# Loading the last stage's inputs during the last image's layer 3, into tiles that earlier stages leave

## The chip, the cores and the metric

The kernel runs on one core of one Trainium2 chip. The metric is device time in microseconds, and the median of several runs counts. TensorE (PE) multiplies into PSUM, VectorE (DVE) and ScalarE (ACT) do the elementwise work, GpSimd (POOL) does small corrections and some copies, and SyncE (SP) issues nearly all DMA transfers, which run on 16 DMA engines.

## The reference

The input is x, 16 images of 64 channels, 128 x 128, float32. Four residual layers follow each other; `gn` is a group norm without parameters over 32 groups of two channels.

```python
x = x + conv1x1(gram(gn(x)) @ gn(x))            # layer 0: a 64 x 64 Gram matrix per image
x = x + |sobel_x(gn(x))| + |sobel_y(gn(x))|     # layer 1: depthwise
x = x + conv3x3(shift(gn(x))) + b               # layer 2: a quarter of the channels shifted left, one right
v = conv1x1(conv3x3(gn(x), w_bin)) + b1         # layer 3
mean, var = v.mean((0, 2, 3)), v.var((0, 2, 3)) # over all 16 images
v = (v - mean) * rsqrt(var + 1e-5) * gamma + beta
x = x + clip(leaky_relu(v), 0, 255)
```

Layer 3's statistics run over the whole batch. So its final normalisation and addition can only begin when the convolution of the last image is done.

## The kernel before

The work has two parts. The first goes through the images in a software pipeline. A step handles one group of 8 rows of each image half (R = 8, NS = 8 groups per image), and each step has four quarters q. In one step the pipeline works on up to four images: `Gram` (the Gram matrix of a later image), `Front` (layers 0 and 1), `Layer2` and `Layer3`. They start at fixed offsets: image b has its layer 3 in steps 35 + 8b to 43 + 8b. All engines are wrapped in `InOrder` (line 72), so each engine keeps the order in which the program issues.

During the last image's layer 3 (from step 155 on) no other stage has work left. A group i of that layer takes one step:

- q = 0: PE forms the shared product and half of the others, from `v3`.
- q = 1: PE forms the other half; ACT normalises the next group from the layer's inputs (`x3` tiles, a ring of 10 of which an image holds 8); SP stores the previous group's `y` to `y_d` in four transfers (line 835).
- q = 2: DVE adds the products into a `y` tile (ring of 2, line 839), then forms differences of the next group, for which PE waits.
- q = 3: more differences, and ACT squares y for the statistics.

Layer 3's input of every image was stored to the DRAM tensor `x3_d` earlier, by layer 2. All SBUF pools of this part are opened in a `with ExitStack() as ph` block (line 157), so their memory is free again when it ends.

The second part, here called the end, starts with a short chain of small operations on the sums (`mv`, `pm_bn`, `sc`, `sh`). Then it streams over everything: for each of 64 pieces it loads y and the layer's input, applies scale, shift and relu on ACT, clips and adds on DVE, and stores the result. The pieces have 16 rows of 128 floats per partition, so each transfer moves 128 partitions x 8,192 bytes. The tiles come from a pool `io` of its own, with six buffers of each kind, opened after the block has ended; the loads run four pieces ahead:

```python
for n in range(4):
    fetch(n)
for n, (b, q) in enumerate(parts):
    fetch(n + 4)
    yt, rt = loaded.pop(n)
    act.activation(yt, yt, AF.Relu, bias=sh, scale=sc)
    dve.scalar_tensor_tensor(rt, yt, 255.0, rt, op0=ALU.min, op1=ALU.add)
    sp.dma_start(whole(out[b].rearrange("c h w -> (c h w)"), q), rt)
```

SP issues both loads and stores, in this order. In the profile the lines of both parts have one number, 72, that of the wrapper, so groups are told apart by their tiles: `y_d<-y` is a y store of layer 3, `yt<-y_d` and `rt<-x_d` are the loads of the end, `out<-rt` its stores.

Of the kernel before, what the change touches and what calls it, by code (L numbers as in the profile page):

```python
# [15 lines left out]
P = 128  # L16
# [91 lines left out]
def tile_kernel(ctx: ExitStack, tc: tile.TileContext, x, cw_h, w2_t, b2, wbin_t, w1_t, b1, gamma, beta, consts, out):  # L108
# [48 lines left out]
    with ExitStack() as ph:  # L157
        wpool = ph.enter_context(tc.tile_pool(name="wpool", bufs=1))
        xin = ph.enter_context(tc.tile_pool(name="xin", bufs=2))
        work = ph.enter_context(tc.tile_pool(name="work", bufs=2))  # L160
        ring = ph.enter_context(tc.tile_pool(name="ring", bufs=2))
        stp = ph.enter_context(tc.tile_pool(name="stp", bufs=2))
        ps_two = ph.enter_context(tc.tile_pool(name="ps_two", bufs=2, space=PSUM))
        ps_one = ph.enter_context(tc.tile_pool(name="ps_one", bufs=1, space=PSUM))
        ps_po = ph.enter_context(tc.tile_pool(name="ps_po", bufs=1, space=PSUM))
        ps_g = ph.enter_context(tc.tile_pool(name="ps_g", bufs=1, space=PSUM))
        ps_sm = ph.enter_context(tc.tile_pool(name="ps_sm", bufs=1, space=PSUM))

        def sv(name, n=1):
            return small.tile([P, n], F32, tag=name, name=name)  # L170

        def cols(o):
            return slice(o * C, (o + 1) * C)

        last = [1]

        def small_product(dst, wt, src):

            for o in (1 - last[0], last[0]):
                pe.matmul(dst[cols(o)], wt[:, cols(o)], src, start=True, stop=True)  # L180
            last[0] = o


        bank = ps_sm.tile([P, 512], F32, name="bank")
        turn = [0]

        def sm(n, rows=P):
            if n > 8:
                return bank[0:rows, P:P + n]
            turn[0] = (turn[0] + 1) % 16  # L190
            return bank[0:rows, 8 * turn[0]:8 * turn[0] + n]
# [3 lines left out]
        xw = wpool.tile([P, W // 2, C + 1, 2], F32, name="xw")  # L195
        nc.gpsimd.memset(xw[:, :, C, :], 1.0)

        xh = wpool.tile([P, 3, R + 2, W + 2], F32, name="xh")
        nc.gpsimd.memset(xh, 0.0)
        junk = wpool.tile([P, R * W], mybir.dt.bfloat16, name="junk")  # L200
        wbd = wpool.tile([P, P], F32, name="wbd")
        nc.gpsimd.memset(wbd, 0.0)

        w2 = wpool.tile([P, 3, 3, P], F32, name="w2")
        w3 = wpool.tile([P, 3, 3, P], F32, name="w3")
        nc.gpsimd.memset(w2, 0.0)
        nc.gpsimd.memset(w3, 0.0)
        for slot, i, o, ky in TO_SLOTS:
            nc.scalar.dma_start(w2[i * C:(i + 1) * C, slot, :, o * C:(o + 1) * C], w2_t[:, ky])

        wm = wpool.tile([P, 3, P], F32, name="wm")
        for n in range(2):
            o = 1 - single(TO_SLOTS, n)[0]
            nc.vector.tensor_copy(wm[:, :, cols(o)], w2[:, n, :, cols(o)])
        w0 = wpool.tile([P, P], F32, name="w0")
        nc.gpsimd.memset(w0, 0.0)

        wb = work.tile([P, R + 1, W + 2], F32, tag="u", name="wb")
        wb = flat(wb)[0:C, 0:9 * C].rearrange("p (y x c) -> p y x c", y=3, x=3)
        w1 = work.tile([P, R, W + 2], F32, tag="e", name="w1", bufs=1)[0:C, 0, 0:C]  # L220
        nc.scalar.dma_start(wb, wbin_t)
        nc.scalar.dma_start(w1, w1_t)
        for ky in range(3):
            pw = sm(3 * C, rows=C).rearrange("p (k c) -> p k c", k=3)
            for kx in range(3):
                nc.tensor.matmul(pw[:, kx, :], wb[:, ky, kx, :], w1, start=True, stop=True)
            for slot, i, o, kk in TO_PAIRS:
                if kk == ky:
                    nc.vector.tensor_copy(w3[i * C:(i + 1) * C, slot, :, o * C:(o + 1) * C], pw)

        packed = {}
        for name, w, table in (("pk2", w2, TO_SLOTS), ("pk3", w3, TO_PAIRS)):
            nc.vector.tensor_add(w[:, 2], w[:, 0], w[:, 1])
            packed[name] = wpool.tile([P, 2, C], F32, name=name)
            for n in range(2):
                o, i = single(table, n)
                for kx, half in ((1, i), (0, 1 - i)):
                    nc.vector.tensor_copy(
                        packed[name][half * C:(half + 1) * C, n], w[i * C:(i + 1) * C, n, kx, o * C:(o + 1) * C]
                    )  # L240

        diffs, twins = {}, {}
        for name in ("d2", "d3"):
            diffs[name] = wpool.tile([P, 2, CP, W + 2], F32, name=name)
            nc.gpsimd.memset(diffs[name], 0.0)
            twins[name] = wpool.tile([P, 2, CP, W + 2], F32, name=f"q{name}")
            nc.gpsimd.memset(twins[name], 0.0)


        chains = []  # L250

        def tick():
            for c in list(chains):
                if next(c, chains) is chains:
                    chains.remove(c)

        def rstd(mE, eps):

            me = sv("me", 2)
            dve.tensor_copy(me, mE)  # L260
            nv = sv("nv")
            dve.scalar_tensor_tensor(nv, me[:, 0:1], me[:, 0:1], me[:, 1:2], op0=ALU.mult, op1=ALU.subtract)
            var = sv("var")
            dve.tensor_scalar(var, nv, -1.0, eps, op0=ALU.mult, op1=ALU.add)
            sd = sv("sd")
            act.activation(sd, var, AF.Sqrt)
            yield
            r0 = sv("r0")
            dve.reciprocal(r0, sd)

            e = sv("e")
            dve.scalar_tensor_tensor(e, var, r0, r0, op0=ALU.mult, op1=ALU.mult)
            dve.tensor_scalar(e, e, -0.5, 1.5, op0=ALU.mult, op1=ALU.add)
            r = sv("r")
            dve.tensor_mul(r, r0, e)
            return r, me[:, 0:1]

        def coefficients(st, put, back=None):

            s2 = sv("s2", 2)  # L280
            dve.tensor_reduce(s2, st, axis=AX.X, op=ALU.add)
            yield
            pm = sm(2)
            small_product(pm, k("gmean"), s2)
            yield
            r, mean = yield from rstd(pm, GN_EPS)
            co = sv("co", 2) if back is None else sv("co2", 6)
            dve.tensor_copy(co[:, 0:1], r)
            dve.scalar_tensor_tensor(co[:, 1:2], mean, -1.0, r, op0=ALU.mult, op1=ALU.mult)
            if back is not None:  # L290

                dve.reciprocal(co[:, 2:3], r)
                dve.tensor_mul(co[:, 3:4], co[:, 2:3], k("left"))
                dve.tensor_mul(co[:, 4:5], co[:, 2:3], k("right"))
                dve.tensor_add(co[:, 5:6], mean, back)
            put(co)


        lead = {}

        def gram_chain(b, pg):

            gs = stp.tile([P, C + 1], F32, tag="gs", name=f"gs_{b}", bufs=1)
            dve.tensor_copy(gs, pg)
            if b > 1:
                yield
            gd = sm(C + 1)
            small_product(gd, k("same"), gs)
            yield
            g = stp.tile([P, C + 1], F32, tag="g", name=f"g_{b}", bufs=1)  # L310
            dve.tensor_scalar_mul(g, gd, 1.0 / HW)
            mu = g[:, C:C + 1]
            st = sv("st0", 2)
            dve.tensor_copy(st[:, 0:1], mu)
            junk0 = stp.tile([P, C], F32, tag="junk0", name=f"junk0_{b}", bufs=1)
            dve.scalar_tensor_tensor(
                junk0, g[:, 0:C], 1.0, k("Id"), op0=ALU.mult, op1=ALU.mult, accum_out=st[:, 1:2]
            )
            if b > 1:
                yield  # L320
            pm = sm(2)
            small_product(pm, k("gavg"), st)
            yield
            r, mean = yield from rstd(pm, GN_EPS)

            vv = sv("vv", 5)
            dve.tensor_scalar_mul(vv[:, 0:1], mu, -1.0)
            dve.tensor_sub(vv[:, 1:2], mu, mean)
            dve.tensor_copy(vv[:, 2:3], mu)
            dve.tensor_sub(vv[:, 3:4], mu, mean)  # L330
            dve.tensor_scalar_mul(vv[:, 4:5], mean, -1.0)
            if b > 1:
                yield
# [6 lines left out]
            if b > 1:  # L340
                yield
# [5 lines left out]
            for s in range(2):  # L347
                dve.tensor_add(cs[:, s, :], pc, g[:, 0:C])
# [645 lines left out]
```

## Time and profile before

| | |
|---|---|
| median of 3 runs | 2853.81 us (2851.17 to 2856.24) |
| profiled execution | 2855.78 us, span 2854.0 us |
| PE busy | 2238.3 us, 78% of the span |
| DVE / ACT / POOL busy | 2193.6 / 2101.5 / 886.8 us |
| moved by DMA | 685.91 MB, mean 240 GB/s |
| loads and stores of the end | 64 + 64 + 64 transfers of 1,024 KB |
| y stores of layer 3 | 512 transfers of 128 KB |

The busy shares are averages over two parts that differ. The page's 40 slices, 71 us each, show this: PE is busy in nearly all of the first 33, and not at all in the last six, where the DMA engines are. A line of the groups names engine, operation, output and inputs, the count, the busy time, the mean of one, and the idle time before it with what ended it. A line of the waits names who waited for whom, the total, the count and the longest. In the DMA listing "to landing" is the time from a transfer's issue to the arrival of its data.

### The profile page before, as it was taken

The page shows a single profiled execution, that of the slowest core. Times are in us where ns is not written, and L with a number is a line of the kernel's source. Part 1 is how long each engine was busy: PE and PEld are TensorE (multiplying, and loading weights), DVE is VectorE, ACT ScalarE, POOL GpSimd, SP SyncE. Part 2 cuts the span into 40 slices and gives each one's busy share as a digit, 9 for nine tenths or more (in the row PEclk, how much of TensorE's full clock was granted, in tenths as well). Part 3 has the DMA queues.
Part 4 walks back from the last instruction along what each step waited for, and adds up shares of the span by engine and source line. Part 5 has one row for each costly group of instructions (what it writes and reads, how often), then busy time and mean ns, then how long its engine had stood idle before and what let it go on. Part 6 is the DMA issues. An engine that isn't in the chain of part 4 may idle for free. (4 is left out here: it accounts for less than half of the span.)

```text
span 2854.0 us, 45849 instructions
## 1 busy us (share of the span) xinstructions
PE 2238.3 (78%) x14772; PEld 1166.6 (41%) x14772; DVE 2193.6 (77%) x3694; ACT 2101.5 (74%) x3107; POOL 886.8 (31%) x1326
## 2 busy tenths in 40 slices
PE   3568899999999999999999999999999992000000
PEld 2333444545463635363635453566666640000000
DVE  3999999898989898989898989999995333332332
ACT  4666779888889898888898979899996674222222
POOL 1045434343434343434333434444443300000000
PEclk8678999999999999999999999999999996555555
DMA  6788978888888888888888867888877528999999
GB/s 164 191 221 225 234 199 239 215 224 215 220 216 221 218 221 217 216 216 216 220 220 217 214 178 193 211 209 209 211 199 185 145 71 320 426 426 426 426 426 394
DMA packets 661229, 685.91 MB, mean 240 GB/s; under 512 B 58672, under 2 KB 587072, under 8 KB 636416
## 3 DMA queue, kind: packets, MB, share of 16 engines
q1 hardware_dynamic: 635008, 614.41, 72.7%
q0 software_dynamic: 24576, 68.12, 9.8%
q8 instruction: 119, 1.95, 0.3%
q14 instruction: 118, 0.97, 0.1%
q10 hardware_dynamic: 1408, 0.46, 0.1%
HBM read 346.23 MB, written 268.44 MB: 215 GB/s over the span
## 5 line engine op out<-in xcount | busy, mean ns | idle before, releaser
L72 PE MATMUL two<-d,w 128*64 128x508 f32 (+2 forms) x2560 | 890.5, 586 | 0.0
L72 PE MATMUL two<-d,wi 128*64 128x508 f32 (+3 forms) x1536 | 619.7, 577 | 0.0
L72 POOL DMA_DIRECT2D qd<-d x512 | 270.3, 530 | 868.9 <-issue 312.7
L72 PE MATMUL two<-qd,pk 128*64 128x512 f32 (+1 forms) x1024 | 518.9, 588 | 6.3 <-DMA qd<-d 5.8
L72 POOL TENSOR_SCALAR edges<-v,co 64x8 f32<-64x8 f32 x512 | 355.3, 694 | 358.9 <-ACT v L72 266.7
L72 PEld LDWEIGHTS two<-d,w 128*64 128x64 f32 x2560 | 306.2, 136 | 275.7 <-issue 188.8
L72 PE MATMUL po<-x,abd 128*64 128x512 f32 x1024 | 367.9, 628 | 56.9 <-ACT xh L72 55.9
L72 DVE TENSOR_TENSOR d<-v 128x512 f32<-128x512 f32 (+1 forms) x512 | 346.8, 680 | 76.2 <-issue 36.9
L72 DVE SCALAR_TENSOR_TENSOR rt<-yt,rt 128x2048 f32<-128x2048 f32 x64 | 146.7, 2292 | 321.3 <-DMA rt<-x_d 321.3
L72 PE MATMUL one<-v,w 128*64 128x508 f32 (+2 forms) x1600 | 392.7, 578 | 0.0
L72 PE MATMUL one<-v,wi 128*64 128x508 f32 (+3 forms) x1536 | 391.1, 593 | 0.0
L72 ACT ACTIVATE yt<-yt,sh,sc 128x2048 f32<-128x2048 f32 x64 | 134.1, 2095 | 332.7 <-DMA yt<-y_d 332.7
L72 ACT COPY qd<-d 64x512 f32<-64x512 f32 x512 | 316.0, 617 | 20.9 <-DVE d L72 14.5
L72 DVE SCALAR_TENSOR_TENSOR e<-e 128x1032 f32<-128x1032 f32 (+1 forms) x256 | 313.4, 1224 | 0.0
L72 ACT ACTIVATE xh<-po,co 128x128 f32<-128x128 f32 (+1 forms) x480 | 275.6, 622 | 39.5 <-PE po L72 37.4
L72 PEld LDWEIGHTS two<-d,wi 128*64 128x64 f32 x1536 | 195.8, 135 | 145.8 <-issue 96.3
L72 DVE SCALAR_TENSOR_TENSOR y<-two,c 128x1024 f32<-128x1024 f32 x128 | 156.1, 1220 | 122.7 <-ACT v L72 65.7
L72 POOL TENSOR_SCALAR v<-v,kc 128x9 f32<-128x9 f32 x256 | 245.1, 971 | 12.0
L72 PEld LDWEIGHTS one<-v,w 128*64 128x64 f32 x1600 | 172.7, 137 | 157.1 <-issue 92.6
L72 ACT ACTIVATE v<-x,co 128x512 f32<-128x512 f32 (+2 forms) x368 | 235.6, 707 | 0.0
L72 PEld LDWEIGHTS one<-v,wi 128*64 128x64 f32 x1536 | 164.9, 139 | 152.4 <-issue 106.4
L72 ACT ACTIVATE u<-u 128x1024 f32<-128x1024 f32 x128 | 135.7, 1060 | 96.1 <-DVE u L72 95.8
(136 smaller groups left out, 3455.2 us busy)
## 6 DMA issues: line engine op xcount, KB each, us to landing
xr<-in_x SPq DMA_DIRECT2D x128, 512.0 KB, 6.9
x<-in_x SPq DMA_DIRECT2D x256, 256.0 KB, 4.2
x_d<-u SPq DMA_DIRECT2D x512, 128.0 KB, 3.6
y_d<-y SPq DMA_DIRECT2D x512, 128.0 KB, 4.2
yt<-y_d SPq DMA_DIRECT2D x64, 1024.0 KB, 16.2
rt<-x_d SPq DMA_DIRECT2D x64, 1024.0 KB, 12.3
out<-rt SPq DMA_DIRECT2D x64, 1024.0 KB, 14.4
x_d<-x SPq DMA_DIRECT2D x496, 128.0 KB, 2.5
```

What stands on the lines that cost most here:

```text
L72: return self.tc.keep_in_program_order(call(*args, **kwargs))
```

## The change

The pools are opened in the kernel's own stack instead of the block's, so they stay open to the end; the body of the block moves one level out and is otherwise the same. The pool `io` and the PSUM pool of the statistics are gone; the statistics' product takes a part of the PSUM tile that the small products share. A piece of the end now has 8 rows per partition (N = 8 x 128), so there are 128 pieces, and each transfer moves 128 partitions x 4,096 bytes.

The end's loads go into slots in a queue `room`. Step 155 puts 24 slots into it: eight slices of `xw` and three of `xh`, the buffers of `x`, `xr`, `u`, `e` and `v2`, and a slice each of layer 2's differences and their twins. During the steps that follow, layer 3's inputs are added: three at step 155, then one per step up to step 160. After each quarter of these steps one piece is fetched (two loads on SP) if two slots are there. That makes 16 pieces before the loop ends. After it the last two inputs and the buffers of `y` and `v3` are added and three more pieces are fetched. In the end's loop a piece's two slots go back to the queue, and a fetch follows when more than eight are in it.

```diff
-    with ExitStack() as ph:
-        wpool = ph.enter_context(tc.tile_pool(name="wpool", bufs=1))
...
+    wpool = ctx.enter_context(tc.tile_pool(name="wpool", bufs=1))
...
-        for step in range(8 * (B - 1) + 35 + NS + 1):
+    last_one = NS * (B - 1) + starts[0][1]
+    steps = last_one + NS + 1
+    N = R * W
+    parts = [(b, q) for b in range(B) for q in range(C * HW // P // N)]
+    room, loaded = deque(), deque()
...
+    def rest(pool, tag, shape, bufs, n=None):
+        for m in range(bufs if n is None else n):
+            t = pool.tile([P] + shape, F32, tag=tag, name=f"end_{tag}_{len(room)}", bufs=bufs)
...
+            room.append(t[:, 0:N])
+
+    def slices(t, n):
+        room.extend(t[:, j * N:(j + 1) * N] for j in range(n))
+
+    fetched = [0]
+
+    def fetch():
+        n = fetched[0]
+        if n < len(parts):
+            b, q = parts[n]
+            yt, rt = room.popleft(), room.popleft()
+            sp.dma_start(yt, whole(y_d[b], q))
+            sp.dma_start(rt, whole(x3_d[b], q))
+            loaded.append((yt, rt))
+            fetched[0] += 1
+
+    for step in range(steps):
...
+            if step == last_one and q == 0:
+                slices(xw.rearrange("p w c t -> p (w c t)"), 8)
+                slices(xh.rearrange("p a j w -> p (a j w)"), 3)
+                rest(xin, "x", [R, W], 2)
+                rest(xin, "xr", [C // 8, W], 3)
+                rest(work, "u", [R + 1, W + 2], 2)
+                rest(work, "e", [R, W + 2], 1)
+                rest(ring, "v2", [(R + 1) * W + 2], 3)
+                for t in (diffs["d2"], twins["d2"]):
+                    slices(t.rearrange("p n j w -> p (n j w)"), 1)
+            if step >= last_one and q == 2:
+                n = 3 if step == last_one else 1 if step < last_one + NS - 2 else 0
+                rest(ring, "x3", [2, CP, W], NS + 2, n)
+            if step >= last_one and len(room) > 1:
+                fetch()
...
+    rest(ring, "x3", [2, CP, W], NS + 2, NS + 2 - 3 - (NS - 3))
+    rest(ring, "y", [2, CP, W], 2)
+    rest(ring, "v3", [R + 1, W], 2)
+    while len(room) > 1:
+        fetch()
...
-    ps_sm = ctx.enter_context(tc.tile_pool(name="ps_bn", bufs=1, space=PSUM))
...
-    pm = ps_sm.tile([P, 2], F32, name="pm_bn")
+    pm = sm(2)
...
-    io = ctx.enter_context(tc.tile_pool(name="io", bufs=6))
-    N = 16 * W
...
-    for n in range(4):
-        fetch(n)
-    for n, (b, q) in enumerate(parts):
-        fetch(n + 4)
-        yt, rt = loaded.pop(n)
+    for b, q in parts:
+        yt, rt = loaded.popleft()
         act.activation(yt, yt, AF.Relu, bias=sh, scale=sc)
         dve.scalar_tensor_tensor(rt, yt, 255.0, rt, op0=ALU.min, op1=ALU.add)
         sp.dma_start(whole(out[b].rearrange("c h w -> (c h w)"), q), rt)
+        room.extend((yt, rt))
+        if len(room) > 8:
+            fetch()
```

## The prediction

> **What bounds the kernel now.** I read the page's slices first, then the waits, the DMA issues, and last a table of stretches around the place where the change works. The slices show two regimes: 33 slices led by TensorE, then seven in which only the DMA engines work.
>
> ```profile
> span 2854.0 us, 45849 instructions
> ...
> PE   3568899999999999999999999999999992000000
> ...
> DMA  6788978888888888888888867888877528999999
> GB/s 164 191 221 225 234 199 239 215 224 215 220 216 221 218 221 217 216 216 216 220 220 217 214 178 193 211 209 209 211 199 185 145 71 320 426 426 426 426 426 394
> ```
>
> The table of stretches (us; busy time and count of PE, PEld, DVE, ACT, POOL; PE clock; DMA share; GB/s) cuts the last 552 us:
>
> ```profile
> 2302.00:2318.00 16.00, 15.51 (x67) 4.89 (x65) 6.16 (x16) 12.18 (x22) 0.00 (x0) 1.00 0.27 67
> 2318.00:2334.00 16.00, 16.00 (x68) 5.35 (x66) 4.88 (x8) 12.56 (x21) 0.00 (x0) 1.00 0.28 70
> 2350.00:2370.00 20.00, 19.25 (x80) 6.45 (x76) 5.54 (x9) 14.65 (x26) 0.00 (x0) 1.00 0.25 63
> 2370.00:2376.00 6.00, 0.56 (x2) 0.50 (x2) 2.86 (x14) 1.35 (x3) 0.00 (x0) 0.68 0.58 146
> 2376.00:2400.00 24.00, 0.00 (x0) 0.00 (x0) 9.17 (x4) 9.58 (x5) 0.00 (x0) 0.50 1.02 413
> 2400.00:2600.00 200.00, 0.00 (x0) 0.00 (x0) 61.89 (x27) 55.35 (x27) 0.00 (x0) 0.50 1.01 426
> 2800.00:2848.00 48.00, 0.00 (x0) 0.00 (x0) 13.75 (x6) 12.57 (x6) 0.00 (x0) 0.50 1.01 427
> 2848.00:2854.00 6.00, 0.00 (x0) 0.00 (x0) 0.00 (x0) 0.00 (x0) 0.00 (x0) 0.50 0.09 40
> ```
>
> The reader is to see three stages. To 2370 the last image's layer 3 fills PE and leaves the DMA engines three quarters idle. From 2376 to 2848 they are full without a gap. The last 6 us drain. ACT and DVE wait for loads through the full stage, and SP for stores:
>
> ```profile
> ACT yt L72 <- DMA yt<-y_d: 332.7, 64, 6.1
> DVE rt L72 <- DMA rt<-x_d: 321.3, 64, 6.1
> ...
> SPq L72 <- DMA out<-rt: 342.3, 58, 8.2
> ```
>
> The DMA listing of that stage (KB each, median us from issue to landing):
>
> ```profile
> DMA packets 27610, 201.03 MB, mean 421 GB/s; under 512 B 3072, under 2 KB 3072, under 8 KB 3072
> ...
> out<-rt SPq DMA_DIRECT2D x64, 1024.0 KB, 14.4
> yt<-y_d SPq DMA_DIRECT2D x62, 1024.0 KB, 16.2
> rt<-x_d SPq DMA_DIRECT2D x62, 1024.0 KB, 12.3
> ```
>
> 1 MB at 426 GB/s takes 2.46 us, so a landing after 12 to 16 us means five or six transfers in the queue. All data packets have 8 KB. The end is bytes over rate: 201.0 MB in 472 us.
>
> **The change, part by part.**
>
> *Bytes moved out of the full stage.* A piece is now 8 rows x 128 = 1,024 floats on 128 partitions, 0.524 MB, so a pair of loads is 1.049 MB. Sixteen pairs, 16.8 MB, are issued among the last image's y stores. Left from 2376 on: 201.0 - 16.8 = 184.2 MB. At 426 GB/s that is 432.4 us, 39.6 less. The idle stage can take them: 68 us from 2302 to 2370 at 73% idle is 50 us, and the pairs need 40.
>
> *The packets are halved to 4 KB.* A partition's run in a piece is now 4,096 bytes. The trace has no full stage of such packets, so I bound it from both sides. With 512-byte packets (the loads of xr) the DMA engines are also full, and slower:
>
> ```profile
> DMA packets 2843, 1.73 MB, mean 288 GB/s; under 512 B 56, under 2 KB 2759, under 8 KB 2843
> ```
>
> (stretch 28 to 34 us). Per engine, one of 16: 288 GB/s is 28.4 ns for 512 bytes, and 426 GB/s is 307.7 ns for 8,192. A straight line gives 158.7 ns for 4,096, which is 413 GB/s. The upper bound is 426 (cost tied to the transfer, not to the packet). [...] I take 413: its line rests on two rows of this trace[...]. The halved packets thus give back 13.6 us.
>
> *More, smaller transfers.* There are 384 transfers of 0.5 MB in place of 192 of 1 MB. In the compiled order [...] each DMA waits for the one eight before it; before, the load of rt also waited for the store five transfers back. So 5 MB were in flight, and now 8 x 0.524 = 4.2 MB. [...] A lone 128 KB store lands 2.4 us after its issue; 4.2 MB in flight are 10.1 us of queue. I take nothing. SP issues a transfer in 0.32 to 0.65 us, three per 3.8 us: hidden too.
>
> *ACT and DVE in the end.* 128 of each in place of 64, on 1,024 elements: rows of that width are 1,057 ns (ACT junk<-y) and 1,225 ns (DVE y<-two,c). 135 and 157 us in all, under 446 of DMA. If DMA were not the bound, DVE could hand out a store every 1.2 us, about as fast as a store moves. Nothing.
>
> *The start of the end.* SP's y stores of row group 7 go out from 2370.6 to 2373.2, and the first load follows at 2373.6. The change issues its pairs 16 to 18 there: 3.1 MB, 7.6 us of queue, while ACT and DVE start on pieces already loaded and return the first store after 2375.1 (shift ready) + 1.06 + 1.23 = 2377.4. So the queue is full from about 2376, as before. Nothing. The last transfers are 15 stores of loaded pieces; the drain of 6 us stays.
>
> *SP's queue during layer 3.* POOL issues nothing here (busy 0.00). On SP the pairs stand between y stores, and this is where the change adds a wait. Four pairs (10.2 us at 413) and one group of four y stores (26.3% of 68 us over 33 stores is 0.54 each, so 2.2) come per step of 7.8 us, so the queue falls behind. Ledger: after the old image's last y group has landed (about 2311.5), twelve pairs (30.5) and y groups 0 to 2 (6.5) are queued in turn, so group 2 has landed at about 2348.5. The y ring has two buffers, so DVE's y of group 4, which ran at 2345.9, waits for that: 2.7 us. DVE's differences stand behind it and PE waits for those; PE has about 0.5 us of the shared product as cover. Groups 5 to 7 meet fewer pairs (2, 0, 1). I take +2.2 us. Bounds: 0, if a y store costs 20% less; 5, if one costs 30% more. Slots are not the wait: the first 24 are free since layer 2 and earlier, and the freed inputs of layer 3 are last read by ACT one step before their load. Instruction fetches (four in 68 us) share the fuller engines: 0 to 2 us, I take 0, since five of them in the full stage left no gap there.
>
> *The rest.* The first 2,300 us issue the same instructions on all engines. The statistics' product goes to the shared PSUM bank instead of its own: same instruction, no wait. Open pools cost no instruction.
>
> **Sum.** 2854.0 - 39.6 (bytes) + 13.6 (packets) + 2.2 (y ring) = 2830.2 us of span. The profiled execution took 2855.78 in all, 1.97 over the median 2853.81, so the median comes to 2830.0.
>
> **The rivals.**
>
> 1. *Packets cost nothing more.* The rate stays at 424 to 426. For it: the full stage shows a share of 1.01, so packets overlap a little. Against: the 512-byte row. 2854 - 39.6 + 2 = 2816, or 2816 as a median.
> 2. *The gain is mostly eaten.* The rate is near 400 (460.5 us) and the y ring costs 4 us: 2854 - 472 + 460.5 + 4 = 2846. For it: 4.2 MB in flight instead of 5[...]. Against: 10 us of queue over a 2.4 us transfer.
> 3. *Slower: the queue runs dry in the end.* With eight half-size transfers in flight SP must reissue in time; it decides below 184.2 MB / (472 - 2.2) = 392 GB/s, reached if a transfer took over 10.7 us (4.2 MB / 392 GB/s) from its issue to the next issue in its turn with nothing queued ahead. At 380 GB/s: 484.7 us, so 2854 + 12.7 + 2.2 = 2869. Against: the 2.4 us landing.
> 4. *The loads do not run early.* If SP stood at a slot until layer 3 ended, all 201 MB would go at 413, 486.7 us: 2869. Against: the waits in the compiled order, which name only work that is done by then.
>
> **How the numbers follow.** This kernel's measurement can tell about 0.2% (5.7 us) from no change. Main case, [...] 0 to 5 us of wait: 62%, 2822 to 2838. Rival 1: 20%, 2812 to 2822. Rival 2: 12%, 2838 to 2848. Between rival 2 and no gain: 2%. Rivals 3 and 4: 4% together. The range 2812 to 2842 takes the main case, rival 1 and the nearer part of rival 2. Faster by over 0.2%: 94%; within: 2%; slower: 4%.
>
> **What would show it.** Right: DMA above 0.8 from about 2310 to 2345; a full stage that starts near 2378 at about 413 GB/s with 49,152 packets of 4 KB less the early ones, landings near 10 us for all three kinds, and ends near 2824; one DVE y waiting two or three us for a y store. Wrong: 426 GB/s (rival 1), gaps or a share below 1 in the full stage (rivals 2, 3), a DMA share still near 0.27 up to 2370 (rival 4), several late y (the ledger).

## The result and the profile after

The changed kernel takes 2828.02 us (median of four runs, 2826.34 to 2829.08), beside 2852.49 us for the kernel before in the same series. The ratio is 0.9912, with a 95% interval of 0.9895 to 0.9929: faster by 24.5 us. The predicted 2830.0 was 2 us off. But two terms of its sum were each about 7 us off, with opposite signs; most of the experiments below are about them.

The page after, its slices:

```profile
span 2827.3 us, 46297 instructions
...
PE   4568899999999999999999999999999995000000
...
DMA  6788978888888888888888877888877668999999
GB/s 166 192 219 227 235 199 237 213 232 205 229 209 224 213 221 215 220 216 223 215 221 216 220 183 191 207 207 213 208 209 186 156 201 285 419 420 420 420 420 391
```

The full stage at the end now runs at 420 GB/s, and no slice is nearly empty any more (201 GB/s in the 33rd, where the page before has 71). The table of stretches after (columns as in the prediction):

```profile
2302.00:2318.00 16.00, 15.50 (x67) 4.81 (x65) 4.88 (x8) 12.14 (x21) 0.00 (x0) 1.00 0.85 306
2318.00:2334.00 16.00, 16.00 (x68) 5.57 (x66) 4.88 (x8) 12.54 (x22) 0.00 (x0) 1.00 1.00 341
2334.00:2350.00 16.00, 12.96 (x50) 5.61 (x46) 2.44 (x4) 7.65 (x13) 0.00 (x0) 0.89 1.03 375
2350.00:2370.00 20.00, 16.85 (x64) 5.47 (x65) 6.99 (x12) 12.66 (x22) 0.00 (x0) 0.91 0.61 197
...
2400.00:2600.00 200.00, 0.00 (x0) 0.00 (x0) 69.11 (x58) 69.52 (x57) 0.00 (x0) 0.50 1.03 420
```

Where layer 3 left the DMA engines at a share of 0.27, they are now full up to about 2350. And PE has 12.96 of 16 us in the third line, where it was busy throughout before:

```profile
2334.00:2350.00 16.00, 16.00 (x68) 5.34 (x66) 4.88 (x8) 12.56 (x21) 0.00 (x0) 1.00 0.28 71
```

So the layer itself has become slower. The waits between 2300 and 2380 name the cause:

```profile
DVE y L73 <- DMA y_d<-y: 18.5, 2, 10.1
...
DVE y L73 <- DMA end_x<-y_d: 6.8, 1, 6.8
```

DVE waits for y stores; before, no wait for a store stands in this stretch. Not all of the 18.5 us is lost, since DVE always idles some 5.4 us there for PE and ACT. What is lost is read from the starts of DVE's y (timeline: start, duration, what, idle before it and its releaser). Before, they follow each other every 7.8 us:

```profile
2330.21 1.23 DVE L72 SCALAR_TENSOR_TENSOR y<-two,c 128x1024 f32<-128x1024 f32 x1 [5.39 <-ACT v L72]
...
2338.04 1.23 DVE L72 SCALAR_TENSOR_TENSOR y<-two,c 128x1024 f32<-128x1024 f32 x1 [5.39 <-ACT v L72]
```

After:

```profile
2327.42 1.22 DVE L73 SCALAR_TENSOR_TENSOR y<-two,c 128x1024 f32<-128x1024 f32 x1 [5.38 <-PE two L73]
...
2338.32 1.22 DVE L73 SCALAR_TENSOR_TENSOR y<-two,c 128x1024 f32<-128x1024 f32 x1 [8.46 <-DMA y_d<-y]
...
2350.82 1.23 DVE L73 SCALAR_TENSOR_TENSOR y<-two,c 128x1024 f32<-128x1024 f32 x1 [10.06 <-DMA y_d<-y]
...
2360.07 1.23 DVE L73 SCALAR_TENSOR_TENSOR y<-two,c 128x1024 f32<-128x1024 f32 x1 [6.81 <-DMA end_x<-y_d]
...
2367.89 1.22 DVE L73 SCALAR_TENSOR_TENSOR y<-two,c 128x1024 f32<-128x1024 f32 x1 [5.38 <-ACT v L73]
```

These are groups 2 to 6. An undisturbed step is 7.82 us (the last two). The intervals here are 10.90, 12.50, 9.25 and 7.82, so groups 3, 4 and 5 come late by 3.1, 4.7 and 1.4 us, 9.2 in all. Groups 3 and 4 wait for the stores of groups 1 and 2, for a buffer of the ring: 7.8 us.

Group 5 is another case. Its releaser is listed as a load, but its buffer was free: the last store of group 3 was issued at 2351.7 and landed 5.5 us later, at 2357.2. Its y started when PE had the product ready, and PE was slow. PE had stood idle for 3.25 us behind the second late y; 0.9 us after it began again, at about 2353.6, its granted clock fell to 0.50, and stayed there until 2357.0. The timeline of PE, and two stretches of 2 us (columns as above):

```profile
2352.71 1.18 PE L73 MATMUL two<-d,w 128*64 128x512 f32 x2 [3.25 <-DVE d L73]
...
2358.96 1.01 PE L73 MATMUL two<-d,w 128*64 128x508 f32 x2
```

```profile
2354.00:2356.00 2.00, 1.94 (x6) 0.71 (x8) 0.00 (x0) 1.93 (x5) 0.00 (x0) 0.50 0.88 261
...
2358.00:2360.00 2.00, 2.00 (x12) 0.69 (x10) 0.00 (x0) 0.97 (x2) 0.00 (x0) 1.00 0.91 326
```

Six matmuls fit where twelve do at the full clock, and the last product of group 5 ends at 2359.97, 0.1 us before its y. So a wait of DVE costs more than itself here: PE, which stands idle meanwhile, then works for 3.4 us at half its clock.

To compare kernels free of what happens earlier, I cut each profile at two such rows: the start of y in group 6 of the image before the last, and in group 7 of the last image. Between them lie nine groups, *layer 3's stretch*; from the second row to the span's end is *the end's stretch*.

| | first row | layer 3's stretch | the end's stretch | span |
|---|---|---|---|---|
| before | 2298.54 | 70.8 | 484.7 | 2854.0 |
| after | 2295.77 | 80.0 | 451.6 | 2827.3 |
| difference | -2.8 | +9.2 | -33.1 | -26.7 |

The first column is the same program up to there and differs from run to run (2292.9 to 2301.2 over the profiles of this study). So the change gave 33.1 us at the end and took 9.2 in layer 3.

### The profile page after: what moved, and what is told of

Its sections match the earlier page's. It is cut to its first block, busy times and chain, and to the rows that moved or that the text cites. A ratio compares the mean times of both kernels' runs of the same rounds, so it can differ in the third digit from the quotient of the medians.

```text
span 2827.3 us, 46297 instructions
## 1 busy us (share of the span) xinstructions
PE 2241.5 (79%) x14772; PEld 1157.1 (41%) x14772; DVE 2200.4 (78%) x3758; ACT 2120.5 (75%) x3171; POOL 884.3 (31%) x1326
## 5 line engine op out<-in xcount | busy, mean ns | idle before, releaser
L73 POOL TENSOR_SCALAR edges<-v,co 64x8 f32<-64x8 f32 x512 | 348.8, 681 | 357.9 <-ACT v L73 248.7
L73 DVE SCALAR_TENSOR_TENSOR u<-xh 128x1170 f32<-128x1170 f32 x128 | 175.5, 1371 | 12.2 <-ACT xh L73 9.8
L73 PEld LDWEIGHTS po<-x,abd 128*64 128x64 f32 x1024 | 110.8, 140 | 174.3 <-ACT xh L73 93.1
```

What stands on the lines that cost most here:

```text
L73: return self.tc.keep_in_program_order(call(*args, **kwargs))
```

## The experiments

**Half the pace.** The fetches during layer 3 come after every second quarter only.

```diff
-            if step >= last_one and len(room) > 1:
+            if step >= last_one and q % 2 == 0 and len(room) > 1:
                 fetch()
```

> The fetches during layer 3 come only after quarters 0 and 2, so two pairs per step in place of four. Theory 1 (crowding: SP's queue and the DMA queue fall behind the y stores, and DVE waits for a buffer of the y ring): two pairs are 5.0 us and a y group 2 to 3 us of a 7.8 us step, so DVE's waits for y stores (18.5 us listed in two waits, some 9 us of them on the path) go, and the time falls by 8 to 9 us below the changed kernel, to about 2819 us. Theory 2 (the loads slow the stage in another way, by their bytes or by the shared memory, whatever their spacing): the 16.8 MB are the same, so the last y stays as late and the time stays at 2828 within 3 us.

Measured: 2819.19 us, ratio to before 0.9882 (0.9869 to 0.9896). The starts of y keep their step of 7.82 us, and layer 3's stretch is 70.8 us (2292.90 to 2363.66), as before the change. The DMA engines are full all the same:

```profile
2312.00:2328.00 16.00, 15.86 (x66) 5.57 (x68) 4.88 (x8) 12.51 (x22) 0.00 (x0) 1.00 0.97 328
2328.00:2344.00 16.00, 16.00 (x68) 5.45 (x66) 4.88 (x8) 12.54 (x21) 0.00 (x0) 1.00 0.96 333
2344.00:2364.00 20.00, 19.57 (x82) 6.67 (x78) 5.21 (x9) 14.93 (x26) 0.00 (x0) 1.00 0.97 331
```

With the same 16.8 MB and a DMA share of 0.97, PE is busy again in 16 of 16 us. So the loss is one of spacing, and theory 2 falls. The share doesn't show the difference; the landing of the y stores between 2312 and 2352 does, in the changed kernel and then at half pace:

```profile
DMA to landing us min/median/max: 5.5/8.4/11.0
```

```profile
DMA to landing us min/median/max: 2.6/3.2/3.7
```

The end's stretch is 451.7 us, as with the change.

**A ring of three for y.** The last image's y goes into the buffers of `xr`; the pace is the fast one.

```diff
-                    y = ring.tile([P, 2, CP, W], F32, tag="y", name=f"y_{b}_{i}")
+                    if b + 1 == B:
+                        y = xin.tile([P, C // 8, W], F32, tag="xr", name=f"y_{b}_{i}", bufs=3)
+                        y = y.rearrange("p (s j) w -> p s j w", s=2)
+                    else:
+                        y = ring.tile([P, 2, CP, W], F32, tag="y", name=f"y_{b}_{i}")
...
-                rest(xin, "xr", [C // 8, W], 3)
...
+                rest(ring, "y", [2, CP, W], 2)
```

(One of layer 3's inputs is given free a little earlier, so that 16 pairs go early as before.)

> The last image's y goes into the three buffers of xr, which has no other work left, in place of its own ring of two; the two y buffers join the slots in their stead; the pace stays at four pairs per step. Theory 1 in its narrow form (the depth of the y ring decides): a third buffer gives each y store a step of 7.8 us more, the two late ones were 5 to 9 us late, so DVE waits less than 2 us in all and the time falls by 6 to 9 us to about 2820. If bandwidth alone decides (theory 2), or SP's order holds up something else than y, the waits stay and the time stays at 2828.

Measured: 2819.73 us, ratio 0.9885 (0.9870 to 0.9900); layer 3's stretch 70.8 us, the end's 451.2. Here the crowding stayed:

```profile
2312.00:2328.00 16.00, 15.73 (x66) 5.31 (x64) 5.21 (x9) 12.18 (x20) 0.00 (x0) 1.00 1.03 391
2328.00:2344.00 16.00, 16.00 (x68) 5.54 (x66) 5.24 (x9) 12.18 (x20) 0.00 (x0) 1.00 1.04 404
```

The DMA engines moved even more per microsecond than in the changed kernel, the y stores landed as late (a median of 7.9 us between 2312 and 2352), and no y is late. Two independent remedies, more time between the loads and one more buffer, take away the same 9 us. That shows the wait: the y store lands too late for a ring of two. With it goes the stretch of PE at half its clock.

**POOL issues the early pairs.** Only the issuing engine differs, `pool.dma_start` in place of `sp.dma_start` for the fetches inside the loop.

> The 16 pairs of layer 3's time are issued by POOL, which has no other work then, in place of SP; pace and slots as changed. If the y stores were late because they stand behind the pairs in SP's order and in its queue: SP issues a y group as soon as DVE is done, the DMA engines serve both queues, the y waits go, and the time is about 2820. If the engines' bytes are what delays them: the y waits stay near 9 us and the time at 2828. [...]

Measured: 2831.68 us, ratio 0.9925 (0.9913 to 0.9938). The second expectation is the nearer one: the wait for the y store stays, and the time lies 3.7 us above the changed kernel. Layer 3's stretch is 83.1 us. POOL has no y stores between its fetches, so only the transfer eight back held it (0.6 to 1.9 us before each load from the ninth to the 24th): its first early pair went at 2280.5, in layer 2's last steps, and twelve were out by 2310. The DMA engines were full earlier (a share of 1.05 from 2296 to 2312), and one y bore most of it, 10.6 of the 12.3 us:

```profile
2324.35 1.23 DVE L73 SCALAR_TENSOR_TENSOR y<-two,c 128x1024 f32<-128x1024 f32 x1 [16.36 <-DMA y_d<-y]
```

The next y came 1.8 us late, again with PE at a clock of 0.50 (2326.2 to 2331).

The DMA listing from 2296 to 2372 of this kernel gives a median landing of 2.4 us over all y stores. But of the 12 issued between 2290 and 2330 the median is 13.7, though the loads were in another queue:

```profile
y_d<-y SPq DMA_DIRECT2D x12, 128.0 KB, 13.7
```

So the order of issue on SP is not the only thing that delays a y store; loads that another engine has queued delayed it here too. And the y stores between the pairs on SP, which look like an obstacle, had worked as a brake. POOL with a pace of its own was not tried.

**No early loads.** The two lines of the fetch in the loop are taken out.

> No fetch before the step loop has ended; then 19 pairs at once. Everything else as changed: open pools, small pieces, slots. If the early loads are the whole gain and open pools and slots cost nothing: 201.3 MB at 420 GB/s are 479 us in the full stage, 7 us more than before, and no y wait, so 2853 + 7 = 2860, 32 us above the changed kernel. If slots or open pools cost something by themselves: above 2866. If the small pieces are free: 2853.

Measured: 2861.1 us, ratio 1.0028 (1.0017 to 1.0039). The end's stretch is 491.7 us, 40.1 above the changed kernel: 2.5 us for each of the 16 pairs, which is 1.049 MB at 420 GB/s. So the early loads are the whole gain; without them the change is slower than what it replaced, by the 7 us of its small pieces. Slots and open pools show no cost beside that: layer 3's stretch is 70.8 us, as before.

**Packets alone.** The kernel before, with its own transfers of 1 MB and its pool `io`, but a partition's 8 KB taken in g runs that lie apart in DRAM.

```diff
-        return d.rearrange("(p n) -> p n", p=P)[:, q * N:(q + 1) * N]
+        return d.rearrange("(p g q n) -> p g q n", p=P, g=2, q=NQ)[:, :, q, :]
+
+    def runs(t):
+        return t.rearrange("p (g n) -> p g n", g=2)
...
-            sp.dma_start(yt, whole(y_d[b], q))
+            sp.dma_start(runs(yt), whole(y_d[b], q))
```

(The load of rt and the store likewise; g is 2, 4 and 16.)

> The kernel before, with transfers of 1 MB as they were, but each partition's 8 KB taken as two runs of 4 KB that lie apart in DRAM; early loads, slots, and bytes in flight as before. If the fall from 426 to 420 GB/s is a cost of each packet: 420 GB/s and 479 us in the full stage, 2853 + 7 = 2860. If it comes from the smaller transfers (more completions, 4.2 MB in flight in place of 5): 426 GB/s and 2853. If the straight line through the 512-byte row held: 413 and 2868.

> The kernel before with its 1 MB transfers, each partition's 8 KB taken as four runs of 2 KB apart in DRAM. Two full stages so far give 307.7 ns per 8 KB packet (426 GB/s) and 156.0 per 4 KB (420), a fixed 4.3 ns: then 80.2 ns, 409 GB/s, 201 MB in 492 us, 2853 + 20 = 2873. The prediction's straight line through the 512-byte row gives 84.3 ns, 389 GB/s, 517 us, 2898.

> The same with sixteen runs of 512 bytes. With the fixed 4.3 ns: 23.3 ns per packet, 352 GB/s, 571 us, 2952. If 512-byte packets are slow by themselves, as the row of the loads of xr said: 28.4 ns, 288 GB/s, 698 us, about 3080; then the straight line was the wrong rule between 512 bytes and 8 KB, and not the row.

Measured: 2862.43 us with runs of 4 KB (ratio 1.0032, 1.0019 to 1.0044), 2881.32 with 2 KB (1.0096, 1.0077 to 1.0114), 3015.27 with 512 bytes (1.0565, 1.0546 to 1.0584). The first comes nearest to the 2860 expected for a cost of each packet. The second lies 8 us above the smaller of its two; its end's stretch grew by 23.5 us where 20 were worked out. The third lies between its two. The full stages of the three, in this order:

```profile
2600.00:2800.00 200.00, 0.00 (x0) 0.00 (x0) 60.79 (x27) 54.40 (x26) 0.00 (x0) 0.50 1.03 419
```

```profile
2600.00:2800.00 200.00, 0.00 (x0) 0.00 (x0) 59.61 (x26) 54.40 (x26) 0.00 (x0) 0.50 1.05 407
```

```profile
2600.00:2800.00 200.00, 0.00 (x0) 0.00 (x0) 46.05 (x21) 42.27 (x21) 0.00 (x0) 0.50 1.18 318
```

The 200 us before these give 417, 404 and 316 GB/s. With 8 KB at 426 that is, per packet and engine, 307.7, 156.4, 80.5 and 25.8 ns; an estimate from these is 27 bytes per ns and a fixed part of about 5 ns, 7 for the smallest. The fall from 426 to 419 comes with the packets alone, at transfers of 1 MB; transfers of half the size (the changed kernel, 420) cost nothing more. How far the runs lie apart in DRAM was not varied by itself. In the run of 512 bytes the packets are not at 288 GB/s as in the loads of xr, but at 318.

**A seventeenth pair.** Half pace, and the last two of layer 3's inputs are given free at step 161 in place of after the loop.

> Half pace, and the last two of layer 3's inputs given free at step 161 in place of after the loop, so that a 17th pair goes early. One pair is 2.5 us of the full stage: about 2817, 2 to 3 us below half pace, if the DMA engines (0.97 busy in that run's layer 3) have room for it before the last y stores; if not, 2819 as with half pace.

Measured: 2820.71 us, ratio 0.9882 (0.9867 to 0.9897): nothing over half pace. The end's stretch is 451.2 us where 449.2 was due. From 2364 to 2372, around the last y at 2368.9, the engines were at a share of 0.99 (0.68 at half pace), which suggests that the pair had only moved the queue. So the fetches begin two steps sooner, in slots that layer 1 and the Gram stage have left by then, and the pairs behind move up:

```diff
-            if step == last_one and q == 0:
+            if step == last_one - 2 and q == 0:
                 slices(xw.rearrange("p w c t -> p (w c t)"), 8)
...
+            if step == last_one and q == 0:
                 rest(ring, "v2", [(R + 1) * W + 2], 3)
...
-            if step >= last_one and q % 2 == 0 and len(room) > 1:
+            if step >= last_one - 2 and q % 2 == 0 and len(room) > 1:
```

> The kernel with half pace and 17 pairs, but its first four pairs go in steps 153 and 154, into slots free since layer 1 of the last image. Half pace with 17 pairs filled the DMA engines to 0.99 until the last y stores and gained nothing over 16. If the room in the DMA engines was what the 17th pair lacked: 2.5 us below half pace in the same call, about 2817. If the fetches delay the end of layer 2 (its last stores and twins): 2820 or more.

> Half pace once more, beside the kernel above on one chip: 2819 as before, within 2 us.

Measured: 2818.20 us (ratio 0.9874, 0.9860 to 0.9889) beside 2821.90 for half pace again (0.9882, 0.9866 to 0.9899). The intervals overlap, so the totals alone don't part them. The profiles do: layer 3's stretch is 70.8 us in both, the end's is 449.2 and 451.3 us, the 2 us of a pair less. SP issued three of the first four pairs ahead of the y store at 2297.9, and layer 2's end was not later (14.1 us between the two y before layer 3's stretch in both). Half pace itself came out 2.7 us above its first measurement, a little more than the 2 us allowed. So this kernel has the lowest median of the study, but only the profiles set it apart from half pace and from the ring of three; by their medians they lie 6 to 10 us below the changed kernel.

## Why the prediction was right, and where it was not

- *Bytes moved out of the full stage: right.* 39.6 us were predicted for 16 pairs; 40.1 were measured, at the lower rate, against the kernel without early loads.
- *Packets: right in kind, too large.* The term was +13.6 us, from 413 GB/s (446.0 us for 184.2 MB). It is +6.2: 184.2 MB take 438.6 us at 420. The step that failed is the straight line through the 512-byte row. Its lower end was the stretch of xr's loads, 288 GB/s, while runs of 512 bytes in the end's own pattern reach 318. A line from there gives 157.3 ns and 416 GB/s; measured are 156.0 and 420. The rate near 400 of rival 2 was an estimate that no trace had shown; with packets of 4 KB the stretches of 200 us gave 417 to 420.
- *Smaller transfers: right.* They were taken to cost nothing, and none shows: eight transfers of 0.5 MB in flight keep the engines at a share of 1.03 and 420 GB/s, where transfers of 1 MB with the same packets gave 417 to 419. The landings came out as worked out (10.1 us):

```profile
out<-end_x SPq DMA_DIRECT2D x39, 512.0 KB, 10.0
end_x<-y_d SPq DMA_DIRECT2D x34, 512.0 KB, 9.9
end_x<-x_d SPq DMA_DIRECT2D x34, 512.0 KB, 10.0
```

- *ACT and DVE in the end: right that they are hidden.* ACT's instruction takes 1,237 ns where its row said 1,057; it costs nothing: the full stage stays at a share of 1.03 and 420 GB/s.
- *SP's queue: the right mechanism, far too small.* The ledger gave one late y and +2.2 us. Two y waited for stores, 7.8 us in all, beyond the bound of 5; and a third came 1.4 us late, since PE ran at a clock of 0.50 after its idle time, for which the sum had no term. That is 9.2 us. (The bounds don't follow from the ledger: y stores 20% cheaper leave 0.9 us of it and not 0, 30% dearer make it about 4.) The ledger took the queue's time as pairs at 413 GB/s plus y stores at the 0.54 us that they took in nearly idle engines, 14.2 MB in 37 us, which is 382 GB/s. The stretches above show 341 and 375 at a full share. And it had SP issue a y group when DVE was done with it. SP's own rows in the changed kernel show how late that was:

```profile
2326.76 4.48 SPq L73 DMA_DIRECT2D y_d<-y  x4
...
2338.71 0.37 SPq L73 DMA_DIRECT2D end_x<-x_d  x1
2339.53 4.71 SPq L73 DMA_DIRECT2D y_d<-y  x4
```

  DVE had y of group 1 at 2320.8 and of group 2 at 2328.6; SP came to them at 2326.8 and 2339.5, since four pairs with their waits for the transfer eight back stood before each (loads kept SP waiting for 21.0 us between 2300 and 2362, 2.5 us the longest). After the issue, both took another 7 us to land, where a store in idle engines takes 2.4. Group 1 had landed at 2338.3 and group 2 at 2350.8, where DVE starts. For group 2 the ledger had 2345.7 on this profile's clock, 5 us less. The stretch from the ledger's start (2311.5 - 2.8 = 2308.7) to the landing divides them roughly:

```profile
2308.70:2350.80 42.10, 37.99 (x152) 14.00 (x148) 9.75 (x16) 26.59 (x44) 0.00 (x0) 0.96 1.02 364
```

  The ledger's 14.2 MB at 364 GB/s take 39.0 us, 2 us more than its 37. In the other 3 us the engines moved about 1.1 MB (42.1 us at 364 GB/s are 15.3 MB) that the ledger had not put before the store. This is an estimate; which transfers these were isn't settled.
- *The start of the end, the drain, instruction fetches, the shared PSUM bank: right as a sum*; they were not measured one by one, but the end's stretch holds nothing unexplained (33.1 us measured, 39.6 - 6.2 = 33.4 by the terms).
- *The total* was right partly by luck: -7.4 us on the packets and +7.0 in layer 3's stretch cancel. Of the 2 us between the predicted total and the measured one, 1.3 come from the kernel before, whose median is 2852.49 us in this series and was 2853.81 where the sum began.
- *The rivals:* none happened as a whole. Rival 1 (packets for free) is excluded by the 4 KB run. Of rival 2 the wait for the ring came, and larger than its 4 us, but not its rate of 400. Rival 3 would have left gaps; the full stage has none (a share of 1.03). Of the prediction's own signs of being wrong, the several late y came. The price of rival 4, early loads that do not run early, is what the kernel without them shows: 2861 where 2869 was worked out, the difference being 420 for 413.

## What to carry to other kernels

Idle DMA time in one stage can be filled with the loads of a later, DMA-bound one, and the gain is bytes over rate (here 40.1 us for 16.8 MB in a stage of 420 GB/s). But look at what else uses the queue: a small store whose buffer is needed two steps later can become the bound, and the cure is a pace that leaves time between the loads, or one more buffer (here either took layer 3's stretch from 80.0 to 70.8 us). Set the pace from the stage's own step (here two pairs and a y group in 7.8 us), before the queue decides it. To see whether the pace is right, look at how long the small stores take to land: the share of the DMA engines was about full in the good and in the bad case (0.97 with landings after 3.2 us, 1.00 with 8.4). And count what a wait leaves behind: PE's clock after the gap (here 0.50 for 3.4 us). When a total comes out right, check the terms: cut both traces at the same instruction and compare the pieces.

## What the runs showed of the hardware that was not expected

- With full engines, the rate fell with the packet's bytes as if each packet had a small fixed cost (about 5 ns, the estimate above): 426, 419, 407 and 318 GB/s for packets of 8 KB, 4 KB, 2 KB and 512 bytes in transfers of 1 MB.
- The "share" of the DMA engines rises above one as packets shrink (1.01, 1.03, 1.05, 1.18): it sums the time of the packets, so above one they overlap, and a share near one alone doesn't say how much is moved, or how long a store waits (half pace: 0.97, and stores landed after 3.2 us; the changed kernel: 1.00, and 8.4 us).
- A store in one queue landed after a median of 13.7 us while another queue's loads filled the engines, against 2.4 us in free ones: a queue of its own did not shield it. SP's issue of one such store took up to 3.3 us there, against 0.6.
- After PE had stood idle for 3.25 us, its granted clock was 0.50 for about 3.4 us of its next work, and matmuls that take 0.59 us took 1.06 to 1.12: 1.4 us of layer 3's 9.2. After the idle 2.50 us behind the first late y it was 0.50 from 2340 to 2343 too, but there the next y waited for its store.
